# Layer 2's delta rule: products with beta made ahead of the chunk loop

## The chip, the cores and the metric

The kernel runs on one core of a Trainium2 chip. The metric is the time of one execution on the device in microseconds (us); the time of the kernel before is the median of three runs. One more execution was recorded by the hardware profiler, and all rows and durations below come from that one. The core's engines are called as the profile calls them: PE (TensorE, matmuls; PEld are its weight loads), DVE (VectorE), ACT (ScalarE), POOL (GpSimd), and SP, which issues DMAs.

## The reference, cut to what matters

The model has four layers of attention and feed-forward, for 8 sequences of 256 tokens with 128 features. The change touches the attention of layer 2 alone, a gated delta rule over chunks of 32 tokens, for 4 heads of width 32:

```python
q, k = _l2norm(q), _l2norm(k)
v, k_beta = v * beta[..., None], k * beta[..., None]
A = where(strict_lower, k_beta @ k.T, 0)            # per chunk
attn_inv = inverse of (eye + A)                     # lower triangular, 32 x 32
u = attn_inv @ v
w = attn_inv @ k_beta
def step(S, inp):                                   # over the 8 chunks of a sequence
    q_i, k_i, u_i, w_i = inp
    attn_local = where(incl_lower, q_i @ k_i.T, 0)
    u_t = u_i - w_i @ S
    o_i = q_i @ S + attn_local @ u_t
    return S + k_i.T @ u_t, o_i
S0 = zeros
```

Its output (delta) is mixed with two causal filters of v (a short one of 5 taps, a long one of 64) and with v itself, by gates that a small network computes from x and from statistics of the four paths. The result is normalised, multiplied by a matrix and added to the residual.

## The kernel before, in words

After the first layer the batch is split into two halves, a and b, of four sequences (1024 tokens) each. `run` emits the stages of the halves in a written order; stage 7 is layer 2's attention (`l2_attn`, L1219 to L1476), once for a and once for b. Beside a's stage 7 the program puts the layer 1 experts of half b (L1027 to L1048), beside b's stage 7 the layer 3 experts of half a (L1598 to L1616). The framework's scheduler merges what is emitted: each engine has one queue in order, and the scheduler fixes that order when the program is built, what was emitted first having precedence. `keep_pace` ties the experts to the stage beside them: `step` collects matmuls of the stage as marks, 16 of them in `l2_attn` (8 of the Gram products, L1294, and 8 of the chunk loop, L1367), and the first matmuls of expert unit i of 16 stand on PE behind mark int(0.8 i).

Within `l2_attn` the data of a half are held as [128, 1024] tiles. In the "H" layout (vH, kH, dH) a partition is head and token within the chunk, the columns are sequence, chunk and feature; in the "T" layout (vT, kT, kq) a partition is head and feature. A transpose of 32 x 32 blocks on DVE leads from one to the other. `heads` (L1242) makes a product for each of the four heads, 32 x 32, on four parts of PE's array. An f32 product stands in the profile as two PE records with two weight loads; 4 sequences x 4 heads are then 32 records of each.

The steps, in order:

- Front (L1249 to L1282): normalisation of tokens, projections, causal convolutions, l2 norms, beta = sigmoid.
- Gram products (L1284 to L1302): nb is the mask "below" times beta on DVE (L1286), then times -1 on POOL (L1287). For each of 8 chunks PE makes k k^T and k q^T into one of four PSUM buffers; DVE writes nm = product x nb (L1295) and loc = product x "upto" (L1298).
- FIR (L1310 to L1322): the long filter, 768 records of small matmuls.
- Inverse (L1326 to L1339): 31 rows of forward substitution on DVE, two operations each (L1334, L1335), while PE runs experts. Then an ACT copy (L1336), a DVE transpose (L1338) and an ACT copy with a strided read into inv (L1339), which holds the transposed inverse X.
- Chunk loop (L1356 to L1385): a state of [128, 4 x 32], cleared by a memset. Per chunk: PE ks = k S; DVE r = v - ks (L1369) and r = r x beta (L1370); PE us = X r; DVE copies u (L1375); PE os = q S + loc u, which ACT copies to dH (L1380); PE ss = k^T u; DVE adds it to the state (L1385). The last chunk makes no ss.
- Gates (L1387 to L1476): statistics of the four paths on ACT and DVE, of which those of the filters and v run beside the chunk loop; then the gate network on PE, softmax, mixing, norm, output product, and the addition to x (L1476).

Of the kernel before, what the change touches and what calls it, by code (L numbers as in the profile page):

```python
# [8 lines left out]
F32 = mybir.dt.float32  # L9
# [3 lines left out]
ALU = mybir.AluOpType  # L13
# [3 lines left out]
P = 128  # L17
B, S, D = 8, 256, 128
# [858 lines left out]
class Half(Chip):  # L877
# [341 lines left out]
    def l2_attn(self):  # L1219
# [3 lines left out]
        nc, tc, B, T, NT = self.nc, self.tc, self.B, self.T, self.NT  # L1223
        NC, NB = S // 32, T // 32
        wide = lambda r: r.unsqueeze(2).to_broadcast([P, NB, 32])
        blk = lambda z: z.rearrange("p (j d) -> p j d", d=32)
        by_bn = lambda z: z.rearrange("p (b n d) -> p b n d", n=NC, d=32)
        by_b = lambda z: z.rearrange("p (b s) -> p b s", s=S)
        with ExitStack() as ctx:
# [4 lines left out]
            vH, fsH, flH, dH = big("vH"), big("fsH"), big("flH"), big("dH")  # L1234
            beta = one.tile([P, NB], F32, name="beta", tag="beta")

            with ExitStack() as cm:
                mid = cm.enter_context(self.sb("l2m"))
                vT, kH, loc, inv = big("vT", mid), big("kH", mid), big("loc", mid), big("inv", mid)
                kq = mid.tile([P, 2, T], F32, name="kq", tag="kq")  # L1240

                def heads(out, weights, moving, start=True, stop=True):  # L1242

                    for h in range(4):
                        r = slice(32 * h, 32 * h + 32)
                        mm = nc.tensor.matmul(out[r], weights[r], moving[r], start=start, stop=stop)
                    return mm

                with ExitStack() as c2:  # L1249
                    tmp = c2.enter_context(self.sb("l2t"))  # L1250
                    psum = c2.enter_context(self.ps("l2aps", 4))
                    xn = tmp.tile([P, NT, D], F32, name="xn", tag="xn")
# [4 lines left out]
                    for j, dst in enumerate((vT, kT, qT, bT)):  # L1257
                        for g in range(T // 512):
                            c = slice(512 * g, 512 * g + 512)
                            ps = psum.tile([P, 512], F32, name="proj", tag="m")  # L1260
# [22 lines left out]

                    below, upto = self.const("below", tmp), self.const("upto", tmp)  # L1284
                    nb = big("bT", tmp)
                    nc.vector.tensor_tensor(blk(nb), below.unsqueeze(1).to_broadcast([P, NB, 32]), wide(beta), ALU.mult)  # L1286
                    nc.gpsimd.tensor_scalar(nb, nb, -1.0, None, ALU.mult)  # L1287
                    nm = tmp.tile([P, 32, B, NC], F32, name="nm", tag="xn")
                    for n in range(NC):
                        ps = psum.tile([P, B, 2, 32], F32, name="gram", tag="m")  # L1290
# [13 lines left out]
                with ExitStack() as c2:  # L1304
# [31 lines left out]
                    nc.scalar.copy(nm, xt.rearrange("p s c -> p c s"))  # L1336
                    xc = tmp.tile([P, 32, NB], F32, name="xc", tag="xmat")
                    nc.vector.transpose(xc.rearrange("p c j -> p (c j)"), nm.rearrange("p c s -> p (c s)"))  # L1338
                    nc.scalar.copy(blk(inv), xc.rearrange("p c j -> p j c"))  # L1339

                    fT = big("fT", tmp)
                    short = w["taps"][:, 12:17]
# [10 lines left out]
                wk = cm.enter_context(self.sb("l2gw"))  # L1353


                with ExitStack() as c2:  # L1356
                    tmp = c2.enter_context(self.sb("l2r", 2))
                    psum = c2.enter_context(self.ps("l2rps", 1))
                    st = mid.tile([P, B, 32], F32, name="state", tag="state")
                    nc.vector.memset(st, 0.0)  # L1360
                    for n in range(NC):
                        kn, xn, qn, ln, hn = (by_bn(z)[:, :, n, :] for z in (kq[:, 0, :], inv, kq[:, 1, :], loc, kH))
                        bn = beta.rearrange("p (b n) -> p b n", n=NC)[:, :, n].unsqueeze(2).to_broadcast([P, B, 32])
                        ps = psum.tile([P, B, 32], F32, name="ks", tag="ks")
                        for b in range(B):
                            mm = heads(ps[:, b], kn[:, b], st[:, b])
                        self.step(mm)  # L1367
                        r = tmp.tile([P, B, 32], F32, name="r", tag="r")
                        nc.vector.tensor_tensor(r, by_bn(vH)[:, :, n, :], ps, ALU.subtract)  # L1369
                        nc.vector.tensor_tensor(r, r, bn, ALU.mult)  # L1370
                        ps = psum.tile([P, B, 32], F32, name="us", tag="us")
                        for b in range(B):
                            heads(ps[:, b], xn[:, b], r[:, b])
                        u = tmp.tile([P, B, 32], F32, name="u", tag="u")
                        nc.vector.tensor_copy(u, ps)  # L1375
                        ps = psum.tile([P, B, 32], F32, name="os", tag="os")
                        for b in range(B):
                            heads(ps[:, b], qn[:, b], st[:, b], stop=False)
                            heads(ps[:, b], ln[:, b], u[:, b], start=False)
                        nc.scalar.copy(by_bn(dH)[:, :, n, :], ps)  # L1380
                        if n < NC - 1:
                            ps = psum.tile([P, B, 32], F32, name="ss", tag="ss")
                            for b in range(B):
                                heads(ps[:, b], hn[:, b], u[:, b])
                            nc.vector.tensor_tensor(st, st, ps, ALU.add)  # L1385

                paths = (fsH, flH, dH, vH)  # L1387
                sH = gates.tile([P, NB, 32], F32, name="sH", tag="sH")
# [515 lines left out]
```

## Time and profile before

| | |
|---|---|
| median of three runs (their range) | 2854.66 us (2846.88 to 2856.15) |
| the profiled execution's own time | 2850.54 us |
| its span, first to last instruction | 2848.7 us |
| PE busy, matmul instructions | 2347.8 us, 17346 |
| DVE busy, instructions | 1602.1 us, 3704 |
| ACT busy, instructions | 1022.8 us, 1750 |
| POOL busy, instructions | 318.9 us, 441 |
| mean granted PE clock | 0.883 |

The two executions of layer 2's attention, in us from the span's start:

| | half a | half b |
|---|---|---|
| first Gram product | 1231.8 | 1534.6 |
| row of X copied into inv by ACT begins | 1310.2 | 1601.3 |
| first us of the chunk loop | 1312.2 | 1603.3 |
| end of the last os | 1359.4 | 1646.7 |
| last addition to x (L1476) begins | 1427.3 (the first at 1424.8) | 1709.3 |

How to read it: the 2.0 us between the time of the profiled execution and its span lie outside the instructions. A row of a timeline gives start, duration, engine, line, operation, tiles, count, and in brackets how long the engine was idle before it and what ended that. "issue" stands for idle time in which the engine waited for nothing that the profile shows. A row of waits says who waited for whom, the sum in us, how often, and the longest. A row of busy time by stretch gives the stretch, its length, busy time (and count of instructions) of PE, PEld, DVE, ACT and POOL, the granted PE clock, the DMA engines' busy share and GB/s. A busy PE is not a PE at its peak, since matmuls overlap; starts of successive matmuls say more than durations.

### The profile page before, as it was taken

How to read it: one execution, taken by the hardware profiler on the slowest of the kernel's cores; microseconds unless marked ns; L12 is line 12 of the kernel's file. 1: busy time of each engine (PE TensorE's matmuls, PEld its weight loads, DVE VectorE, ACT ScalarE, POOL GpSimd, SP SyncE). 2: the span in 40 equal slices, each digit the busy share in tenths (PEclk: the TensorE clock that was granted, in tenths of full speed). 3: DMA queues.
4: the chain of work that ended last, by engine and by line, in shares of the span. 5: the costliest groups of instructions: out<-in, count | busy, mean ns of one | idle time of the engine just before them, and what ended most of it. 6: DMA issues, size and time to landing. Idle time of an engine off the chain costs nothing. (4 is left out here: it accounts for less than half of the span.)

```text
span 2848.7 us, 42771 instructions
## 1 busy us (share of the span) xinstructions
PE 2347.8 (82%) x17346; PEld 1553.0 (55%) x17346; DVE 1602.1 (56%) x3704; ACT 1022.8 (36%) x1750; POOL 318.9 (11%) x441
## 2 busy tenths in 40 slices
PE   5784788578789879858895898999698798779999
PEld 3672455367455445445463656666465565545666
DVE  6536443653558988777558754544553644463432
ACT  1021333211349578335542335222234421224322
POOL 0372110047000000000000000000201000210000
PEclk8695799679799989968996899999899899879999
DMA  7133331513200000100010001000221000030100
GB/s 256 22 45 103 103 90 44 194 25 41 79 15 24 9 29 17 31 27 22 12 40 24 17 23 50 1 16 16 59 55 37 27 8 16 26 91 4 43 23 23
DMA packets 103027, 127.27 MB, mean 45 GB/s; under 512 B 15161, under 2 KB 84094, under 8 KB 97726
## 3 DMA queue, kind: packets, MB, share of 16 engines
q1 hardware_dynamic: 61706, 71.56, 8.4%
q10 hardware_dynamic: 28836, 43.28, 4.5%
q0 software_dynamic: 12288, 9.71, 2.5%
q8 instruction: 136, 2.23, 0.3%
q14 instruction: 61, 0.50, 0.1%
HBM read 96.84 MB, written 27.53 MB: 44 GB/s over the span
## 5 line engine op out<-in xcount | busy, mean ns | idle before, releaser
L1610 PEld LDWEIGHTS po<-w_e,hT 128*128 128x128 f32 x2048 | 265.4, 198 | 71.5 <-issue 48.5
L1610 PE MATMUL po<-w_e,hT 128*128 128x128 f32 x2048 | 288.2, 286 | 11.1 <-DVE hT L1604 7.6
L1598 PE MATMUL ph<-x2T,w_e 128*128 128x512 f32 x512 | 264.0, 620 | 5.8 <-ACT hT L1606 4.9
L1606 ACT ACTIVATE hT<-ph,w_l_cols 128x512 f32<-128x512 f32 x192 | 131.3, 686 | 323.1 <-PE ph L1598 319.0
L621 DVE TENSOR_REDUCE nm<-sc 128x3 f32<-128x384 f32 (+1 forms) x192 | 130.4, 689 | 126.4 <-PE sc L619 125.3
L1040 PEld LDWEIGHTS po<-w_e,hT 128*128 128x128 f32 x1024 | 135.3, 197 | 75.9 <-DVE hT L1033 29.4
L658 ACT ACTIVATE pr_e<-scT 128x384 f32<-128x384 f32 (+1 forms) x192 | 111.3, 597 | 171.1 <-PE scT L655 164.2
L1040 PE MATMUL po<-w_e,hT 128*128 128x128 f32 x1024 | 144.8, 286 | 14.3 <-DVE hT L1033 8.6
L1030 PE MATMUL pu<-xnT,w_e 128*128 128x512 f32 x256 | 139.2, 626 | 9.3 <-ACT gs L1032 9.3
L1027 PE MATMUL pg<-xnT,w_e 128*128 128x512 f32 x256 | 138.6, 624 | 0.8 <-ACT prT L223 0.7
L1616 DVE SCALAR_TENSOR_TENSOR x_res<-po,gt,x_res 128x128 f32<-128x128 f32 x256 | 79.4, 358 | 100.8 <-PE po L1610 100.3
L231 PE MATMUL tp<-c_ident,xn 128*128 128x128 f32 x208 | 53.3, 380 | 93.3 <-DVE xn L251 85.6
L500 ACT ACTIVATE gs<-pg 128x512 f32<-128x512 f32 x64 | 38.2, 597 | 249.6 <-PE pg L495 249.6
L1033 DVE SCALAR_TENSOR_TENSOR hT<-pu,w_l_bias,gs 128x512 f32<-128x512 f32 x128 | 95.0, 745 | 57.7 <-PE pu L1030 54.8
L1598 PEld LDWEIGHTS ph<-x2T,w_e 128*128 128x128 f32 x512 | 84.6, 195 | 68.9 <-ACT hT L1606 33.2
L1032 ACT ACTIVATE gs<-pg,w_l_bias 128x512 f32<-128x512 f32 x128 | 87.2, 689 | 96.4 <-PE pg L1027 86.4
L668 PE MATMUL ctx<-pr_e,vz 128*32 128x256 f32 x512 | 106.6, 395 | 2.8 <-ACT pr_e L658 2.8
L1756 DVE TENSOR_TENSOR gw<-sc,dec 128x768 f32<-128x768 f32 x64 | 61.2, 957 | 84.3 <-PE sc L1750 83.9
L513 POOL DMA_INDIRECT l_acc<-eo,idx x64 | 101.9, 1592 | 34.9 <-DVE eo L512 16.9
L617 PE MATMUL sc<-ks,qs 72*128 72x256 bf16 x256 | 75.8, 296 | 28.7 <-DMA ks<-l_parts 17.4
L1046 ACT ACTIVATE ys<-po,pr 128x128 f32<-128x128 f32 x256 | 73.3, 368 | 65.3 <-PE po L1040 64.5
L231 PEld LDWEIGHTS tp<-c_ident,xn 128*128 128x128 f32 x208 | 33.9, 170 | 112.4 <-DVE xn L251 85.5
(604 smaller groups left out, 4998.5 us busy)
## 6 DMA issues: line engine op xcount, KB each, us to landing
l_parts<-sT SPq DMA_DIRECT2D x48, 192.0 KB, 5.0
qs<-l_parts SPq DMA_DIRECT2D x16, 576.0 KB
w_l_wu<-in_l_wu ACTq DMA_DIRECT2D x8, 1024.0 KB
w_e<-in_l_e SPq DMA_DIRECT2D x16, 512.0 KB, 3.4
w_e<-in_l_e ACTq DMA_DIRECT2D x16, 512.0 KB, 4.0
w_e<-in_l_e SPq DMA_DIRECT2D x16, 384.0 KB, 3.2
w_e<-in_l_e ACTq DMA_DIRECT2D x16, 384.0 KB, 3.1
l_parts<-sT ACTq DMA_DIRECT2D x24, 192.0 KB, 4.0
```

The source lines that it names most:

```text
L513: nc.gpsimd.indirect_dma_start(out=accs[h][:, :], out_offset=bass.IndirectOffsetOnAxis(ap=idx[:, j : j + 1], axis=0), in_=eo[:, h, :], in_ ...
L621: nc.vector.tensor_reduce(blocks[:, hp * pr : hp * pr + hp, :], sc[:, :, 0:384].rearrange("p h (k t) -> p h k t", t=P), AX.X, ALU.max, neg ...
L658: nc.scalar.activation(pe, sc[:, :, 0:384], AF.Exp, scale=float(1.0 / np.sqrt(np.float32(8.0))))
L668: nc.tensor.matmul(o, z, pe[:, 0:S], start=(j == 0), stop=False)
L1027: mm = nc.tensor.matmul(pg, wg[:, c], xnT[:, cols], start=True, stop=True)
L1030: self.keep_pace(nc.tensor.matmul(pu, wu[:, c], xnT[:, cols], start=True, stop=True), part)
L1032: nc.scalar.activation(gs, pg, AF.Silu, bias=w["l1_bias"][:, 0, e, k : k + 1])
L1033: nc.vector.scalar_tensor_tensor(hT[:, k, :], pu, w["l1_bias"][:, 1, e, k : k + 1], gs, ALU.add, ALU.mult)
L1040: nc.tensor.matmul(po[:, i, :], hT[:, k, i * P : (i + 1) * P], wd[:, k * P : (k + 1) * P], start=(k == 0), stop=(k == 1),)
L1598: mm = nc.tensor.matmul(ps, we[:, k * P : (k + 1) * P], xnew[:, 512 * g : 512 * g + 512], start=True, stop=True)
L1606: nc.scalar.activation(hT[:, k, :], ps, AF.Relu, bias=bias)
L1610: nc.tensor.matmul(po[:, i, :], hT[:, k, i * P : (i + 1) * P], we[:, (4 + k) * P : (5 + k) * P], start=(k == 0), stop=(k == 3),)
```

## The change

The equations are turned. With X the inverse, u_t = X (beta v) - X (beta k) S. The factor beta goes into X's columns once, as X is stored (on DVE, in place of ACT's copy). From this X beta, the loop makes z (X beta k, transposed, as weights for the product with S) and y = X beta v for two chunks at a time in one PSUM buffer "zy", ahead of the first chunk of each pair; DVE copies z over the place of k in kq, ACT copies y over vT, which are no longer needed by then. None of these depends on the state. What then remains of a chunk is us = z S, u = y - us on DVE, ss = k^T u (now emitted ahead of os), os and the addition to the state. The first chunk takes u = y, and has no products with the empty state, so that no memset is needed; the state after it is a copy of ss. The mark of the first chunk becomes the last product of the first zy, that of the others the last us. The sign of the Gram mask is put on beta (32 columns, DVE) in place of the whole mask (1024 columns, POOL).

```diff
                     nb = big("bT", tmp)
-                    nc.vector.tensor_tensor(blk(nb), below.unsqueeze(1).to_broadcast([P, NB, 32]), wide(beta), ALU.mult)
-                    nc.gpsimd.tensor_scalar(nb, nb, -1.0, None, ALU.mult)
+                    less = tmp.tile([P, NB], F32, name="less", tag="less")
+                    nc.vector.tensor_scalar(less, beta, -1.0, None, ALU.mult)
+                    nc.vector.tensor_tensor(blk(nb), below.unsqueeze(1).to_broadcast([P, NB, 32]), wide(less), ALU.mult)
...
-                    nc.scalar.copy(blk(inv), xc.rearrange("p c j -> p j c"))
+                    nc.vector.tensor_tensor(blk(inv), xc.rearrange("p c j -> p j c"), wide(beta), ALU.mult)
...
+                zT, y = kq[:, 0, :], vT
...
-                    nc.vector.memset(st, 0.0)
                     for n in range(NC):
-                        kn, xn, qn, ln, hn = (by_bn(z)[:, :, n, :] for z in (kq[:, 0, :], inv, kq[:, 1, :], loc, kH))
-                        bn = beta.rearrange("p (b n) -> p b n", n=NC)[:, :, n].unsqueeze(2).to_broadcast([P, B, 32])
-                        ps = psum.tile([P, B, 32], F32, name="ks", tag="ks")
-                        for b in range(B):
-                            mm = heads(ps[:, b], kn[:, b], st[:, b])
+                        if n % 2 == 0:
+                            ps = psum.tile([P, B, 2, 2, 32], F32, name="zy", tag="zy")
+                            for b in range(B):
+                                for j in range(2):
+                                    xn = by_bn(inv)[:, b, n + j, :]
+                                    heads(ps[:, b, j, 0], by_bn(kH)[:, b, n + j, :], xn)
+                                    mm = heads(ps[:, b, j, 1], xn, by_bn(vH)[:, b, n + j, :])
+                            nc.vector.tensor_copy(by_bn(zT)[:, :, n : n + 2, :], ps[:, :, :, 0, :])
+                            nc.scalar.copy(by_bn(y)[:, :, n : n + 2, :], ps[:, :, :, 1, :])
+                        zn, yn, qn, ln, hn = (by_bn(z)[:, :, n, :] for z in (zT, y, kq[:, 1, :], loc, kH))
+                        u = yn
+                        if n:
+                            ps = psum.tile([P, B, 32], F32, name="us", tag="us")
+                            for b in range(B):
+                                mm = heads(ps[:, b], zn[:, b], st[:, b])
+                            u = tmp.tile([P, B, 32], F32, name="u", tag="u")
+                            nc.vector.tensor_tensor(u, yn, ps, ALU.subtract)
                         self.step(mm)
-                        r = tmp.tile([P, B, 32], F32, name="r", tag="r")
-                        nc.vector.tensor_tensor(r, by_bn(vH)[:, :, n, :], ps, ALU.subtract)
-                        nc.vector.tensor_tensor(r, r, bn, ALU.mult)
-                        ps = psum.tile([P, B, 32], F32, name="us", tag="us")
-                        for b in range(B):
-                            heads(ps[:, b], xn[:, b], r[:, b])
-                        u = tmp.tile([P, B, 32], F32, name="u", tag="u")
-                        nc.vector.tensor_copy(u, ps)
+                        if n < NC - 1:
+                            ss = psum.tile([P, B, 32], F32, name="ss", tag="ss")
+                            for b in range(B):
+                                heads(ss[:, b], hn[:, b], u[:, b])
                         ps = psum.tile([P, B, 32], F32, name="os", tag="os")
                         for b in range(B):
-                            heads(ps[:, b], qn[:, b], st[:, b], stop=False)
-                            heads(ps[:, b], ln[:, b], u[:, b], start=False)
+                            if n:
+                                heads(ps[:, b], qn[:, b], st[:, b], stop=False)
+                            heads(ps[:, b], ln[:, b], u[:, b], start=n == 0)
                         nc.scalar.copy(by_bn(dH)[:, :, n, :], ps)
-                        if n < NC - 1:
-                            ps = psum.tile([P, B, 32], F32, name="ss", tag="ss")
-                            for b in range(B):
-                                heads(ps[:, b], hn[:, b], u[:, b])
-                            nc.vector.tensor_tensor(st, st, ps, ALU.add)
+                        if n == 0:
+                            nc.vector.tensor_copy(st, ss)
+                        elif n < NC - 1:
+                            nc.vector.tensor_tensor(st, st, ss, ALU.add)
```

## The prediction

> **What bounds the kernel now.** I read the page for the span, then the busy time by stretch around the two executions of layer 2's attention (one for each half of the batch, a and b), then the timelines of TensorE (PE) and VectorE (DVE) there, the waits, and the instruction queue among the DMAs. The chain of waits reaches back only to about 2000 us, so it says nothing of this stage; the stretches have to.
>
> ```profile
> span 2848.7 us, 42771 instructions
> ...
> q8 instruction: 136, 2.23, 0.3%
> ```
> ```profile
> 1246.60:1269.60 23.00, 14.94 (x780) 13.27 (x778) 12.53 (x38) 3.19 (x6) 0.00 (x0) 0.62 0.15 39
> 1312.10:1359.40 47.30, 38.91 (x1275) 26.51 (x1275) 30.25 (x68) 25.10 (x48) 0.00 (x0) 0.71 0.04 12
> 1359.40:1425.00 65.60, 57.01 (x200) 29.59 (x201) 37.83 (x54) 36.00 (x64) 1.97 (x1) 0.97 0.05 13
> ...
> 1603.30:1646.80 43.50, 33.92 (x1289) 25.68 (x1290) 28.77 (x71) 16.32 (x28) 0.00 (x0) 0.84 0.05 16
> 1646.80:1710.00 63.20, 59.39 (x235) 34.75 (x236) 35.01 (x63) 25.13 (x34) 1.97 (x1) 0.95 0.05 17
> 1710.00:1743.00 33.00, 33.00 (x189) 23.32 (x188) 12.51 (x44) 9.14 (x14) 0.00 (x0) 1.00 0.00 0
> ```
>
> The columns are stretch, length, busy PE, weight loads, DVE, ACT, POOL, granted clock, DMA. Rows 2 and 4 are the chunk loop of a and b (47.3 and 43.5 us for 8 chunks), rows 3 and 5 the gates and output after it. Half a's layer ends at 1425 us, at the same time as the last experts that run beside it, and PE has some 8.6 us of room in row 3. Half b's layer ends at 1710 us, but PE goes on with the other half's experts, 33.00 of 33.00 us busy in row 6, and the next stage of b follows only after them. So time saved in a counts when the chain or PE is shorter; in b only less idle PE counts.
>
> ```profile
> 1345.79 0.29 DVE L1369 TENSOR_TENSOR r<-vH,ks 128x128 f32<-128x128 f32 x1 [0.86 <-PE ks L1246]
> 1346.11 0.29 DVE L1370 TENSOR_TENSOR r<-r,beta 128x128 f32<-128x128 f32 x1
> 1347.14 0.29 DVE L1375 COPY u<-us 128x128 f32<-128x128 f32 x1 [0.73 <-PE us L1246]
> ...
> 1349.53 0.28 DVE L1385 TENSOR_TENSOR state<-state,ss 128x128 f32<-128x128 f32 x1
> ```
>
> One chunk: three trips between PE and DVE, four DVE operations, about 5 us. What PE does in the waits is expert work, queued there by the order of the program.
>
> ```profile
> 1249.02 1.81 PE L1246 MATMUL fl<-vH,fw 32*32 32x32 f32 x127 [0.83 <-issue]
> 1252.34 1.91 PE L1246 MATMUL fl<-vH,fw 32*32 32x28 f32 x128 [1.52 <-issue]
> 1256.07 0.62 PE L1246 MATMUL fl<-vH,fw 32*32 32x24 f32 x29 [1.81 <-issue]
> ```
>
> This row decides most. In the FIR products, independent small matmuls like those of the chunk loop, PE runs about 128 of them and then stands up to 1.8 us with nothing to wait for. With their weight loads that is 256 instructions. The page's instruction queue fits: 2.23 MB in 136 packets is 16.4 KB each, and PE's 2 x 17346 instructions over 136 packets are 255 each. The packet starts in the trace lie 3.3 to 3.9 us apart in this stretch, and nowhere in the run closer than 3.3. A stream of small matmuls is therefore bound at 3.3 to 3.9 us per 128 records, not by the 14 ns each that PE takes (32 records of "us" in 0.45 us).
>
> **The change part by part.** Each f32 product is two records, so 4 sequences x 4 heads are 32 records a chunk, and each step below is per half.
>
> *Sign on beta.* The front of the stage stands on DVE:
>
> ```profile
> DVE nm L1295 <- POOL bT L1287: 3.0, 1, 3.0
> DVE nm L1295 <- PE gram L1246: 2.0, 1, 2.0
> ```
>
> (half a; b has the first line alike without the second.) The 2.77 us POOL operation goes; a DVE one on 32 columns comes (0.14 us, as beta + 1 in L1280). That frees 2.8 us, but the Gram products are late next: four buffers hold 128 records, and the rest needs the next block of instructions. In a, the last Gram product already made DVE wait 2.0 us; starting the second batch earlier by 2.8 us cannot bring a block closer than 3.3 us after the last. I take 1.5 us (ends 0.5 and 2.8). PE has almost nothing to do then, so this counts in both halves: 3 us.
>
> *Beta into the inverse.* L1339 was an ACT copy with a strided read:
>
> ```profile
> L1339 ACT COPY inv<-xc x2: 1968/1976/1983, 1310.2 to 1601.3; 128x1024 f32<-128x1024 f32 x2
> ```
>
> DVE does it with beta. A product of this size with a broadcast is 1.22 us (L1403); a strided side cost L1295 0.37 against 0.27 for L1298, so 1.2 to 1.7. I take 1.4, a gain of 0.6 us; the ends are a gain of 0.8 and, with one 1.2 us statistic queued ahead on DVE, a loss of 0.9. It also waits no longer for a busy ACT.
>
> *The loop's operations.* Gone: ks (8 x 32 records), us in its old form (256), 32 of os for the first state, and on DVE 8 x 0.29 for r, 8 x 0.29 for r x beta, 8 x 0.29 for the copy of u, one of seven adds turned into a copy, and the memset of 0.17. New: z 256 and y 256 records, 7 x 32 for us, 7 subtractions of 0.29 on DVE; four zT evictions of 256 columns on DVE (0.29 for 128, 0.67 for 512 columns in L221: 0.42 each) and four of y on ACT, about 0.4 each, between the 0.27 us of L1380 for 128 and the 0.59 of L223 for 512 columns. DVE, with the inverse: 7.1 us before; 2.0 + 1.7 + 1.4 = 5.1 after. PE: 256+256+512+224 = 1248 records before, 256+256+224+480+224 = 1440 after, so +192, or +2.7 us at 14 ns.
>
> *The chain per chunk.* Three trips become two (us to u, ss to state), and ss goes ahead of os, whose 64 records fill a wait. From the timeline: 0.45 us, 0.3, 0.29, 0.3, then 0.45, 0.3, 0.29, 0.2: some 2.6 us bare. With the experts' pieces between, 3.2; eight chunks and 2.5 us for the first z and y give 28 us by chain alone.
>
> *What is late next.* Here the Trainium skill speaks: its page "Runtime: NRT & Kernel Launch", section on instruction fetch mechanics, says that PE's instructions come in blocks of 256 while the current block executes, and that crossing a block is mostly hidden. By that the 192 extra records cost 2.7 us and the loops could come near 28 us: 19 + 15 us off the two. The rows above say otherwise for small matmuls: up to 1.8 us of open stall per block. I go by the row. 1440 records are 2880 instructions, 11.25 blocks, 37 to 42 us at 3.3 to 3.75 us, before any expert work lies between. Before, the loop of a held 1275 records, 10.0 blocks, 33 to 37 us: b's 43.5 us were already near that, and one wait of 1.2 us in it has "issue" as its cause. A rule of "TensorE: Matmul & The Clock Gate" (section "Wait — 56ns, not 53.3ns?") speaks against the change too: a small matmul's start costs 25 ns at least, 4.8 us for the 192; the 14 ns of this trace hold instead, with products on different parts of the array.
>
> With 50 expert records left between, 11.6 blocks at 3.6 us: I take 42 us for each loop (ends 37 and 46). Before, each loop held about 13.5 us of experts (in a 48 of 0.11 and 19 of 0.43, start to start at full clock); with one wait fewer per chunk and z and y in the others I expect 8, so 5.5 us of experts move behind the loop.
>
> *Sum, by what PE does.* Loop of a before: 1208 x 0.014 + 13.5 = 30.4 us of work, so 16.9 of 47.3 us were idle or at half clock; b: 30.5, so 13.0. After, at 42 us: 20.2 + 8, so 13.8 lost. Half a: 16.9 - 13.8 = 3.1 less loss, - 2.7 for the new records, + 2.1 for the front and the inverse; of the 8.6 us of room in row 3, 0 to 3.6 can be used, since the tail now starts 7.4 us earlier (5.3 + 2.1) and its end isn't the limit. I take 1.8: 4.3 us gained. Half b: 13.0 - 13.8 - 2.7 + 2.1 = -1.4, and 0 to 3 of the 3.8 us left in row 5: +0.1 at the middle. Together 4.4 us: span 2844, profiled time 2846 where it had 2850.54. Against the median of 2854.66 that is 2850. What comes later keeps its work; the program's scheduling lays its order out anew, which no row prices: 4 us either way, as far as the two executions' equal loops differ (47.3 and 43.5). The marks that pace the experts don't bind: when a's inverse was done, 8 of the 16 units beside it had begun, and the first mark that moves is unit 10's.
>
> **The rivals.**
> *The chain is all.* Fetching hides as the page says; loops of 32 us lose 4 each. Then a gains 16.9 - 4 - 2.7 + 2.1 + 3.6 = 15.9, b 13.0 - 4 - 2.7 + 2.1 = 8.4: 2830. For it: clocks of 0.71 and 0.84 in the loops, PE waits for DVE of 5.6 and 7.3 us in them. Against: the FIR rows. Chance 0.13.
> *Fetch at its quickest.* Blocks 3.3 us apart, loops of 37.5 us, lost 9.3: a 16.9 - 9.3 - 2.7 + 2.1 + 1.8 = 8.8, b 13.0 - 9.3 - 2.7 + 2.1 = 3.1: 2843. For: five of six blocks in the second FIR stretch came at 3.3 to 3.8. Against: in the two loops only one block of some twenty came within 3.4 us of the last. Chance 0.21.
> *Fetch takes more than it gives (slower).* Its place is the loop of b and the stretch to 1743. If the scheduling puts few experts between, PE stands in the stalls: loop 46 us with 4 of experts, 21.8 lost. Then b is 13.0 - 21.8 - 2.7 + 2.1 + 3 = 6.4 later, a 16.9 - 21.8 - 2.7 + 2.1 + 3.6 = 1.9: 2863. It decides from about 44 us with under 6 us of experts between, where the sum passes zero. For: the stall already in b's loop; z and y come in bursts of 128, one block each. Against: list order still fills PE's waits. Chance 0.26.
> *The change doesn't reach the end*, as in the sum: main case, chance 0.40.
>
> **How the numbers follow.** About 0.3% (8.6 us) is what a measurement of this kernel can tell from no change. The main case gives 2850, with its own range 2846 to 2858. The first two rivals are the faster chance, 0.34 (the part of the second within 0.3% and the main case's part beyond it cancel); same 0.40; slower 0.26, with the new order of later layers in it. 2836 to 2864 leaves out most of the first rival and the far end of the third, about 2 in 10.
>
> **What would show it.** DVE's wait for POOL at L1295 is gone, a wait of about 1 to 2 us for Gram stays. The loop from first zy to last os takes 39 to 46 us per half; PE waits with cause "issue" in it, up to 1.8 us each, and instruction packets 3.3 to 3.9 us apart. Fewer expert records lie in it than 1275 - 1208 = 67 in a. Half a's output at about 1420, the end of the experts beside b, with all shifts, 3 to 7 us before 1743. Wrong if loops fall under 37 us, if no "issue" waits appear, or if the end of the experts beside b moves by more than 10 us.

## The result and the profile after

The change made the kernel slightly slower: 2859.26 us at the median of 20 runs (2852.46 to 2866.32), against 2854.70 us for 20 runs of the kernel before (2843.84 to 2859.60). The ratio is 1.0026 with a 95% interval of 1.0015 to 1.0036. The medians differ by 4.6 us; the ratio, which is taken over all the runs, stands for 7.4 us. The forecast was 4.4 us faster. The profiled execution took 2860.8 us.

The page of the changed kernel, first line and instruction queue:

```profile
span 2858.4 us, 43539 instructions
...
q8 instruction: 139, 2.28, 0.3%
```

768 instructions and 3 packets more: 384 matmul records (17730 where there were 17346), 192 per half as counted, with as many weight loads. Busy time by stretch of the changed kernel (same columns as before), rows 1 and 3 the chunk loops of a and b, rows 2 and 4 what follows each:

```profile
1310.20:1356.80 46.60, 31.57 (x1469) 24.02 (x1469) 27.00 (x54) 21.51 (x37) 0.00 (x0) 0.71 0.04 13
1356.80:1425.00 68.20, 59.02 (x203) 31.07 (x204) 39.07 (x64) 36.80 (x63) 1.97 (x1) 0.92 0.04 12
1608.60:1651.10 42.50, 26.59 (x1468) 22.29 (x1467) 25.12 (x52) 15.08 (x26) 0.00 (x0) 0.72 0.02 5
1651.10:1714.00 62.90, 59.67 (x256) 34.80 (x250) 36.01 (x69) 25.41 (x34) 1.97 (x1) 0.97 0.05 17
```

The loops take 46.5 and 42.6 us where they took 47.2 and 43.4: one round trip between PE and DVE less per chunk has bought 0.7 and 0.8 us. Of the 1469 and 1468 records, 1440 are the layer's own, so 29 and 27 are experts, where there were 67 and 81. PE is busy for 7.3 us less in each loop, and in b the granted clock has fallen from 0.84 to 0.72.

What PE waited for in the changed kernel, first half a's loop, then half b's (from some 5 us ahead of each loop on; of the 2.5 us for hT, 0.9 lie ahead of b's):

```profile
PE zy L1246 <- issue: 7.3, 4, 2.7
PE os L1246 <- issue: 3.4, 2, 1.8
PE pu L1030 <- ACT gs L1032: 2.8, 1, 2.8
PE us L1246 <- issue: 1.3, 1, 1.3
```
```profile
PE zy L1246 <- issue: 9.0, 5, 2.4
PE os L1246 <- issue: 3.6, 4, 1.3
PE ph L1609 <- ACT hT L1617: 2.5, 2, 1.6
PE ss L1246 <- issue: 0.8, 1, 0.8
```

Before, PE waited there for DVE, 5.6 us in a; these two rows of a's waits are the larger part of it.

```profile
PE us L1246 <- DVE r L1370: 2.3, 2, 1.6
...
PE os L1246 <- DVE u L1375: 1.8, 3, 0.7
```

The waits for DVE are down to fractions of a us, and 12.0 and 13.4 us of "issue" stand in their place. The packets of the instruction queue start at 1311.4, 1318.5, 1322.6, 1326.4, 1329.7, 1333.2, 1336.8, 1340.6, 1344.1, 1348.6 and 1352.8 in a's loop. The first step, 7.1 us, holds the 2.8 us wait for ACT; the others are 3.3 to 4.5 us. The stalls keep the same step: they end at 1332.07, 1335.81, 1339.54, 1343.00 and 1346.73, and between each of these times and the next PE's records in the trace, matmuls and weight loads together, number exactly 256. PE's timeline shows one such place:

```profile
1333.06 0.65 PE L1246 MATMUL ss<-u,kH 32*32 32x32 f32 x32
1333.51 0.31 PE L1246 MATMUL os<-u,loc 32*32 32x32 f32 x8
1333.62 0.31 PE L1246 MATMUL os<-state,kq 32*32 32x32 f32 x8
...
1335.81 0.27 PE L1246 MATMUL os<-u,loc 32*32 32x32 f32 x4 [1.85 <-issue]
...
1336.85 0.65 PE L1246 MATMUL us<-state,kq 32*32 32x32 f32 x32 [0.18 <-DVE state L1396]
```

The profile shows no wait for a result in the 1.85 us.

At the front, DVE's wait for POOL (3.0 us in each half) is gone; in a the only wait of that kind left is this row, where the Gram products were 2.0 us late before.

```profile
DVE nm L1296 <- PE gram L1246: 1.0, 1, 1.0
```

Then where is the loss? In the experts that run beside a. One line's instructions on PE, their output products from 1300 us to 1445 us (the two times are the first and last start), before and after:

```profile
L1040 PE MATMUL po<-w_e,hT x192: 272/275/582, 1300.1 to 1422.5; 128*128 128x128 f32 x192
```
```profile
L1040 PE MATMUL po<-w_e,hT x168: 272/275/582, 1299.7 to 1437.3; 128*128 128x128 f32 x168
```

They end 15 us later, although a's own layer ends 3 us earlier (its last output product starts at 1423.8, not 1426.8). Half b's next layers need the results of these experts. The first Gram product of half b comes at 1540.8 where it came at 1534.6. Counted from the first projection of a's layer, which starts at a slightly different time in every execution, that is 342.4 us where it was 335.1: 7.3 us late. From there to the end of the experts beside b it is 217.0 us where it was 212.1, another 4.9 us. Then comes the feed-forward of half b's layer 2 (last product in L1213): from its end to the end of the span it is 1074 us where it was 1077. So the loss lies between a's layer and that point, and nothing is lost behind it.

### The profile page after: what moved, and what is told of

Its sections match the earlier page's. It is cut to its first block, busy times and chain, and to the rows that moved or that the text cites. A ratio compares the mean times of both kernels' runs of the same rounds, so it can differ in the third digit from the quotient of the medians.

```text
span 2858.4 us, 43539 instructions
## 1 busy us (share of the span) xinstructions
PE 2345.0 (82%) x17730; PEld 1554.5 (54%) x17730; DVE 1601.6 (56%) x3680; ACT 1029.7 (36%) x1762; POOL 313.1 (11%) x439
## 5 line engine op out<-in xcount | busy, mean ns | idle before, releaser
L1040 PEld LDWEIGHTS po<-w_e,hT 128*128 128x128 f32 x1024 | 136.4, 199 | 77.1 <-DVE hT L1033 33.4
L1040 PE MATMUL po<-w_e,hT 128*128 128x128 f32 x1024 | 145.8, 287 | 13.7 <-DVE hT L1033 11.5
L1030 PE MATMUL pu<-xnT,w_e 128*128 128x512 f32 x256 | 138.4, 623 | 12.9 <-ACT gs L1032 12.9
L1027 PE MATMUL pg<-xnT,w_e 128*128 128x512 f32 x256 | 137.2, 619 | 0.0
L1046 ACT ACTIVATE ys<-po,pr 128x128 f32<-128x128 f32 x256 | 72.9, 367 | 55.2 <-PE po L1040 54.2
```

Source lines behind the costliest of these rows:

```text
L1027: mm = nc.tensor.matmul(pg, wg[:, c], xnT[:, cols], start=True, stop=True)
L1030: self.keep_pace(nc.tensor.matmul(pu, wu[:, c], xnT[:, cols], start=True, stop=True), part)
L1040: nc.tensor.matmul(po[:, i, :], hT[:, k, i * P : (i + 1) * P], wd[:, k * P : (k + 1) * P], start=(k == 0), stop=(k == 1),)
```

## The experiments

Theory A: the small products are bound by their instruction blocks, so the shorter chain cannot shorten the loop, and the experts that stood in the old loop's waits are pushed behind it, where they end late. Theory B: the loss comes from the added instructions wherever the experts stand. Theory C: it comes from something beside the loop (the front, a new order of instructions in the layers behind it). A loop is counted from the first us (in the changed loops zy) to the end of the last os. "Experts' end", "a's end" and "b's Gram" in the table are starts of the last expert product, a's last output product and b's first Gram product, from the first projection of a's layer, in one execution of each kernel.

| kernel | ratio, 95% interval | loops a, b (us) | blocks in the built loops | expert products in the built loops | experts' end | a's end | b's Gram |
|---|---|---|---|---|---|---|---|
| before | 1 | 47.2, 43.4 | 10.0, 10.1 | 33, 40 | 223.0 | 227.3 | 335.1 |
| the change | 1.0026, 1.0015 to 1.0036 | 46.5, 42.6 | 11.5, 11.5 | 14, 13 | 238.9 | 225.4 | 342.4 |
| sign alone | 0.9979, 0.9964 to 0.9995 | 44.7, 42.9 | 10.0, 10.1 | 33, 40 | 219.7 | 224.0 | 331.9 |
| change without sign | 1.0027, 1.0014 to 1.0041 | 47.6, 42.6 | 11.5, 11.5 | 14, 13 | 238.5 | 225.0 | 342.0 |
| three trips, shortened | 0.9979, 0.9965 to 0.9993 | 39.7, 39.5 | 9.6, 9.8 | 23, 32 | 217.4 | 215.8 | 333.3 |
| more products | 1.0020, 1.0001 to 1.0039 | 49.1, 48.3 | 11.5, 11.7 | 34, 49 | 225.2 | 229.1 | 335.4 |
| z and y joined | 0.9944, 0.9920 to 0.9967 | 33.4, 35.7 | 9.4, 9.5 | 12, 14 | 220.9 | 207.4 | 324.4 |
| change, seven ties | 1.0016, 0.9998 to 1.0033 | 56.2, 56.7 | 12.0, 12.2 | 45, 58 | 224.4 | 232.5 | 338.3 |
| joined, seven ties | 1.0004, 0.9988 to 1.0020 | 57.2, 55.2 | 10.0, 10.2 | 46, 58 | 223.8 | 231.9 | 335.1 |
| sign alone, seven ties | 0.9985, 0.9973 to 0.9998 | 59.9, 59.5 | 10.4, 10.6 | 59, 75 | 213.7 | 235.2 | 334.3 |
| change in a alone | 1.0011, 0.9997 to 1.0025 | 46.7, 42.4 | 11.5, 10.1 | 14, 40 | 238.3 | 224.8 | 341.8 |
| change in b alone | 0.9979, 0.9967 to 0.9991 | 45.2, 39.9 | 10.0, 11.5 | 33, 13 | 221.0 | 224.9 | 328.2 |
| change, one tie | 1.0073, 1.0046 to 1.0099 | 52.3, 55.3 | 11.8, 12.1 | 36, 53 | 230.6 | 229.9 | 345.4 |

Blocks are products x 2 records x 2 instructions / 256; an expert product is two records too.

**The sign alone.** The kernel before with only this:

```diff
-                    nc.vector.tensor_tensor(blk(nb), ..., wide(beta), ALU.mult)
-                    nc.gpsimd.tensor_scalar(nb, nb, -1.0, None, ALU.mult)
+                    nc.vector.tensor_scalar(less, beta, -1.0, None, ALU.mult)
+                    nc.vector.tensor_tensor(blk(nb), ..., wide(less), ALU.mult)
```

> The kernel before with the sign on beta alone. PE's queue stands in the same order as before in the Gram products, the FIR and both chunk loops. My theory (the slowdown comes from the chunk loop, which holds more blocks of PE instructions and fewer experts): the front of the stage is 2 to 4 us shorter in each half and both loops stay at 47 and 43 us, so 4 to 6 us faster than before, about 2849. Rival (something in the front, or the mere new order of later layers, made the change slow): no gain, or 3 us and more slower.

2844.48 us against 2849.62: 5 to 6 us faster, as expected. From first Gram product to first FIR product it takes 12.6 and 11.5 us where it took 14.9 and 13.9.

**The change without the sign.** The change with those lines undone:

```diff
-                    nc.vector.tensor_tensor(blk(nb), ..., wide(less), ALU.mult)
+                    nc.vector.tensor_tensor(blk(nb), ..., wide(beta), ALU.mult)
+                    nc.gpsimd.tensor_scalar(nb, nb, -1.0, None, ALU.mult)
```

> The change with the sign put back on POOL as before, so the loop's edits (z and y, two trips, no empty state, beta in the inverse) alone. PE's queue has the change's order. If the two parts add up: the sign alone gave 0.21%, the whole change costs 0.26%, so this one is 8 to 14 us slower than before (0.3 to 0.5%). If the front's gain is lost in the changed kernel because something else comes late there: as slow as the change, 4 to 5 us over before.

2859.62 us against 2852.99, ratio 1.0027, the same as the whole change: the second of the two cases, and the parts don't add up. The front does take 12.9 and 14.0 us again, some 2 us more than in the change (10.9 and 11.8), but the experts' end stays at 238.5. So within the change the sign is worth nothing that can be measured, though alone it is worth 5 us. That half b then waits for the experts, which a shorter front doesn't move, fits this, but is not shown by itself.

**Three trips, shortened.** The sign, beta in the inverse, ss ahead of os and no products with the empty state, but ks, us and ss as before, without z and y. Against the loop of before:

```diff
-                        nc.vector.tensor_tensor(r, r, bn, ALU.mult)
...
+                        r = by_bn(vH)[:, :, n, :]
+                        if n:
+                            ps = psum.tile([P, B, 32], F32, name="ks", tag="ks")
...
```

> The sign, beta in the stored inverse, no products with the empty state and ss ahead of os, but no z and y: r = v - k S, u = X beta r, three trips a chunk as before. By the built order each loop then holds 592 small products (before 604, the change 720), 9.6 and 9.8 blocks of 256 PE instructions, and 23 and 32 expert products, 9.5 and 9.0 us of work (before 33 and 40, 13 us; the change 14 and 13, 6.3 and 4.1 us). My theory: loops of about 40 us, PE time lost in them about 14 us each against 16.9 and 13.0 before; with the front's 5 us some 6 to 9 us faster than before, 2846 to 2849. Rival (the shorter chain is what counts): no faster than the kernel with the sign alone.

2843.65 us against 2849.62, at the near end of what was expected and no better than the sign alone, as the rival had it. The loops are 39.7 and 39.5 us with three trips per chunk, 7 and 3 us shorter than the change's with two, and have 0.4 and 1.6 us of "issue". So three trips at 9.6 blocks are shorter than two trips at 11.5. b's Gram, though, came no earlier than with the sign alone, so the shorter loop in a did not show in the time; why, stays open.

**More products.** The kernel before with each us product of six chunks made twice (the first result is overwritten by the same value), so that the loop has 700 small products, near the change's 720.

```diff
-                            heads(ps[:, b], xn[:, b], r[:, b])
+                            for _ in range(2 if n < 6 else 1):
+                                heads(ps[:, b], xn[:, b], r[:, b])
```

> The kernel before with us made twice in six of eight chunks (the second time over the first, same values): 96 products more a loop, 700 in place of 604, 11.5 and 11.7 blocks as in the change, but with 34 and 49 expert products (13.9 and 15.3 us) still in the loops and POOL's sign as before. If the count of small products alone makes the change slow: 8 to 11 us slower than before (1.5 blocks of 3.6 us in each half), 2863 to 2866. If it is the experts that the change drives out of the loops: only the 1.3 us of PE work a half and some stall, 2 to 6 us slower, 2857 to 2861.

2859.16 us against 2849.62, 9.5 us by the medians and 5.7 by the ratio of 1.0020, whose interval of 0.3 to 11 us covers both forecasts. The trace says more. The loops grew by 2 and 5 us, the experts stayed in them (34 and 49), the experts' end is 2.2 us later and b's Gram within 0.3 us of before. 9 us were lost only later, in the feed-forward of half b's layer 2: 34.3 us from the end of the experts beside b to its last product, where it was 25.6. PE's products stand there, and up to the end of the program, in the same order as before. What differs is the granted clock (the first row is the kernel before, the second this one, the third the change in half a alone, below):

```profile
1746.40:1772.00 25.60, 20.84 (x111) 14.22 (x110) 13.58 (x41) 21.62 (x28) 5.10 (x5) 1.00 0.20 70
1747.00:1781.30 34.30, 29.53 (x111) 20.40 (x110) 14.13 (x41) 23.91 (x33) 5.13 (x5) 0.73 0.16 53
1745.50:1779.10 33.60, 29.11 (x112) 20.22 (x111) 13.59 (x41) 23.53 (x32) 5.13 (x5) 0.74 0.17 54
```

So added instructions alone do not move the experts, which speaks against B for half a. What this execution lost, it lost to the clock in a later layer; why the clock was low there, and whether the other executions lost time in the same place, is not known.

**z and y joined.** The change, with k and v of a chunk side by side, so that one product with 64 columns makes both; z is then transposed on DVE. 592 small products in place of 720.

```diff
+                    kv = mid.tile([P, 2, B, NC, 32], F32, name="kv", tag="kv")
+                    for j, z in enumerate((kH, vH)):
+                        nc.scalar.copy(kv[:, j].rearrange("p b n d -> p (b n d)"), z)
...
-                                    xn = by_bn(inv)[:, b, n + j, :]
-                                    heads(ps[:, b, j, 0], by_bn(kH)[:, b, n + j, :], xn)
-                                    mm = heads(ps[:, b, j, 1], xn, by_bn(vH)[:, b, n + j, :])
-                            nc.vector.tensor_copy(by_bn(zT)[:, :, n : n + 2, :], ps[:, :, :, 0, :])
+                                    mm = heads(ps[:, :, b, j, :], by_bn(inv)[:, b, n + j, :], kv[:, :, b, n + j, :])
+                            nc.vector.tensor_copy(zH, ps[:, 0].rearrange("p b j d -> p (b j d)"))
+                            nc.vector.transpose(zT[:, n * B * 32 : (n + 2) * B * 32], zH)
```

> The change, but z and y come from one product of 64 columns (X beta as weights, k and v side by side, copied there by ACT during the inverse), and DVE transposes z: 592 small products a loop in place of 720, 9.4 blocks in place of 11.5. Expert products in the loops stay few (12 and 14, 5.2 and 4.4 us). If blocks of instructions set the loop's length: loops of 34 to 37 us where the change has 46 and 42, and 8 to 12 us faster than the change, 2847 to 2851. If displaced experts are all that costs and the blocks don't matter: as slow as the change, 2857 to 2860.

2834.41 us against 2849.62, ratio 0.9944: faster than both kernels, and the fastest of all. By the ratios it is 23 us faster than the change, where 8 to 12 were expected. Its loops and what follows a's:

```profile
1304.10:1337.60 33.50, 25.54 (x1209) 20.08 (x1210) 27.80 (x58) 20.32 (x36) 0.00 (x0) 0.80 0.05 16
1337.60:1404.00 66.40, 57.45 (x203) 30.68 (x204) 38.42 (x62) 37.62 (x61) 1.97 (x1) 0.95 0.04 13
1587.00:1622.70 35.70, 25.97 (x1214) 20.91 (x1213) 26.34 (x56) 14.96 (x26) 0.00 (x0) 0.76 0.02 4
```

It has as few experts in its loops as the change, and the same two trips. On PE only the number of products, and with it of blocks, is smaller: 9.4 blocks instead of 11.5, and the loops are 13 and 7 us shorter, although DVE has the transposes on top. 9.4 blocks in 33.4 us are 3.55 us each, the spacing of the packets. The waits of PE in a's loop are mostly for data again, "issue" is down to 1.7 us:

```profile
PE ss L1246 <- DVE u L1385: 2.2, 3, 1.2
PE us L1246 <- DVE state L1400: 1.7, 2, 1.4
PE os L1246 <- issue: 1.3, 1, 1.3
```

The experts take as long behind the loop as in the change (80.0 us, 1337.6 to 1417.6), but the loop ends that much earlier: their last product is at 220.9, near the 223.0 of before, and a's layer ends 20 us earlier.

**Ties.** Three kernels in which seven expert products per half are tied in the built order behind one chunk each, so that the experts stand between the chunks again. The ties add no waits; they only fix the order on PE.

```diff
+    def pin(self, inst, unit, place):
+        m = self.pins.get((unit, place)) if self.pinned else None
+        if m is not None:
+            dep = mybir.DependencyInfo(mybir.DependencyClass.NoSync, mybir.DependencyReason.DATA)
+            self.tc.add_manual_dep(self.pace[m], inst.ins.name, dep, reason="experts between the chunks")
...
+                        self.pin(mu, G * e + g, f"k{k}")
...
+                    self.pin(mo, G * e + g, "po")
```

The marks are numbers 9 to 15, one per chunk after the first.

> The change, but the program ties expert products of the other half between the chunks: marks 9 to 15 of the loop stand on PE behind products of expert units 8 to 10 (half a) or 5 to 7 (half b). By the built order the loops hold 45 and 58 expert products, 18.2 and 19.2 us of work, where the change has 14 and 13 (6.3 and 4.1 us); small products stay 720, blocks go from 11.5 to 12.0 and 12.2. My theory (the experts that the loop no longer takes are what makes the change slow, and they fit into the stalls between blocks): loops 43 to 48 us, the last experts beside a end near 1425 instead of 1437.6, 8 to 14 us faster than the change, so 3 to 9 us faster than before. Rival (blocks alone): 1 to 4 us slower than the change.

The change with seven ties: 2859.35 us against 2852.99, ratio 1.0016, where 8 to 14 us less than the change was expected. By the ratios it is 3 us faster than the change, so both forecasts missed. The experts did come back to 224.4, but the loops grew:

```profile
1303.00:1359.20 56.20, 45.08 (x1531) 31.11 (x1531) 31.92 (x61) 28.63 (x54) 0.00 (x0) 0.82 0.06 18
1598.10:1654.80 56.70, 45.40 (x1558) 34.54 (x1557) 30.30 (x67) 19.11 (x32) 0.00 (x0) 0.82 0.04 13
```

with these waits as the longest in a's loop (the line numbers of this kernel are higher; L1048 is L1030 of the change):

```profile
PE pu L1048 <- ACT gs L1052: 2.8, 1, 2.8
PE po L1060 <- DVE hT L1053: 2.0, 1, 2.0
PE us L1267 <- issue: 1.9, 2, 1.2
```

Now the chain stands behind the experts, with the experts' own waits for ACT and DVE in it.

> Joint z and y product (592 small products a loop) together with the same ties: 46 and 58 expert products in the loops (19 us each), 10.0 and 10.2 blocks. My theory: loops of 38 to 42 us, PE almost without stall in them, 2 to 6 us faster than the joint product alone, so 17 to 22 us under before. If the joint loop's room is used up already or the ties delay its chain: no faster than the joint product alone, or up to 5 us slower than it.

The joined kernel with the ties: 2854.34 us, some 17 us slower by the ratios (1.0004 and 0.9944) than without, outside both forecasts, for the same reason: 57.2 and 55.2 us of loop.

> Control: the kernel before with the sign on beta and the same ties. Its loop took 13 us of experts by itself; with the ties 25 us, in 10.4 and 10.6 blocks. If ties help only where the loop had lost its experts: within 3 us of the kernel with the sign alone, or slower, as the chain of three trips now waits for experts. If ties help any kernel: 5 us and more faster than the sign alone.

The control, the sign alone with the ties: 2847.50 us, ratio 0.9985, near the sign alone. Its loops are 15 and 17 us longer than the sign alone's, with 59 and 75 expert products in them, and most of what is lost there comes back behind: the experts end 6 us earlier, and b's Gram is 2.4 us later.

**Half by half.** The whole change in one half's layer, the other half's layer as before.

```diff
+                if self.tag == "a":
                     with ExitStack() as c2:
...
+                else:
+                    with ExitStack() as c2:
...
```

The first branch is the loop of the change, the second that of before; the sign and the store of X are switched in the same way, and "b" takes the place of "a" in the second kernel.

> The whole change in half a's layer alone; half b's layer is that of the kernel before. If the loss is made in half a (five to seven us by which the change's trace shows half b's Gram products late, because the experts beside a end 15 us later), this kernel is 5 to 8 us slower than the kernel before (ratio 1.0018 to 1.0028) and its trace has half b's first Gram product 5 to 9 us later than before, counted from the start of half a's layer; half b's loop stays at about 43 us. If half a is neutral and all comes from half b, it is within 2 us of before.

2855.87 us against 2851.44: 1.0011, less than expected at the middle, with the lower end of the forecast inside its interval. The trace has what was expected: b's Gram at 341.8, 6.7 us late, and b's loop at 42.4 us. It also has 8 us at the low clock in half b's feed-forward (the third row under "More products"), with the products in the order of before; that part of its loss is not the late experts'.

> The whole change in half b's layer alone; half a's layer is that of the kernel before. If each half carries its own loss, the trace has half b's first Gram product where it was before and the end of the experts beside b 4 to 6 us later, and the time is 3 to 5 us above before (ratio 1.0010 to 1.0018). If the loss is all made in half a, it is within 2 us of before. A sum of the two halves' changes far from the whole change's 7 us would say that the newly laid order of later layers has a hand in it.

2845.58 us against 2851.44: 0.9979, 6 us faster than before and outside both cases. From b's Gram to the experts' end it is 212.7 us, within 0.6 us of before; b's loop takes 39.9 us with 9.8 us of "issue", in the whole change 42.6 with 13.4, in the same form. What it gained lies ahead of b's layer (b's Gram at 328.2), where the code is that of before but PE's order is not quite (328 of the 380 records from a's end to b's Gram match), and where the granted clock was 0.92 and 1.00 (1426 to 1470 and 1470 to 1500 us) against 0.88 and 0.94. So the 4.9 us that half b lost in the trace of the whole change are not a fixed price of it.

**One tie.** The change with one tied expert product per half, which leaves 36 and 53 expert products in the loops. In the table of ties:

```diff
-    5: {(8, "po"): 9, (9, "k0"): 10, (9, "k1"): 11, (9, "po"): 12, (10, "k0"): 13, (10, "k1"): 14, (10, "po"): 15},
...
+PINS = {5: {(9, "k0"): 9}, 9: {(5, "o3"): 9}}
```

> The change with one expert product per half tied behind the loop's first chunk, so that the built order has 36 and 53 expert products in the two loops, near the 33 and 40 of the kernel before, where the change has 14 and 13. If the displaced experts alone make the loss and the seven ties of the earlier kernel were only too many, it is 3 to 8 us faster than the change, at or a little below the kernel before, with loops of 48 to 52 us. If the added instructions make the loss wherever the experts stand, the loops grow by as much as the experts take (50 to 56 us) and the time stays within 2 us of the change (ratio 1.0015 to 1.003).

2871.76 us against 2851.44 (six runs): 1.0073, the slowest, and a miss of both theories' times. The loops are 52.3 and 55.3 us, as the second expected; the experts end 8 us earlier than in the change, but a's end is 4.5 us later, and b's Gram comes at 345.4, 3 us later than in the change. So here experts that end earlier did not bring b's Gram forward. What makes this kernel the slowest stays open.

## Why the prediction was wrong, step by step

- *Blocks bind the small products.* Right. "Issue" stalls of up to 2.7 us, packets 3.3 to 4.5 us apart, exactly 256 instructions from stall to stall, and the loop follows the number of blocks once the chain is shorter: the joined kernel with 9.4 blocks shows it. That the fetch is mostly hidden, as the Trainium skill's page "Runtime: NRT & Kernel Launch" has it in its section on instruction fetch mechanics, would have given loops near 28 to 32 us; measured were 46.5 and 42.6. For this stream the row was the better guide.
- *Loop of 42 us.* b's was 42.6, a's 46.5. In a, 11.5 blocks took 4.0 us each; without the 2.8 us for which one expert product inside waited for ACT, with the chain behind it, 3.8, near b's 3.7. That b's loop came so close is in part luck: the same loop took 39.9 us in the kernel with the change in b alone.
- *Front, 1.5 us a half.* Too small: 4.0 and 2.1 us in the change. The Gram products hardly became late: DVE waits 1.0 us for them in a, where it had waited 2.0. It did not count in the end, as the kernel without the sign shows.
- *14 ns a record.* Too much at the full clock. The 0.45 us for 32 records of us take in the last record's own 0.19; their starts are 8 ns apart where the granted clock was 1.0, and 14 where it was 0.5. At the full clock the 192 new records are 1.6 us and not 2.7, too little to turn the sum.
- *8 us of experts left in each loop, 5.5 us pushed out.* 14 and 13 expert products were left, 6.3 and 4.1 us by the same durations (0.22 us for a po product, 0.86 for a wide one), so 7 and 9 us were pushed out. The trace has z and y products among the chunk's own instead (those that start at 1347.08, for one).
- *"Of the 8.6 us of room in row 3, 0 to 3.6 can be used".* This step failed, and with it the sign of the forecast. The sum took PE's idle time behind a's loop for room that the pushed-out experts could fill, and half a's own layer for the thing to be shortened. But that idle time was the experts' own: of the 8.6 us, 7.7 were waits of expert products for DVE and ACT; ahead of the longest, DVE was at the mixing of the gates (L1459, L1461). These are PE's longest waits behind a's loop (to 1425 us), before and after:

```profile
PE po L1040 <- DVE hT L1033: 3.7, 1, 3.7
PE pu L1030 <- ACT gs L1032: 2.1, 2, 1.4
PE po L1040 <- ACT ys L1046: 1.9, 1, 1.9
```
```profile
PE po L1040 <- DVE hT L1033: 5.2, 2, 4.9
PE pu L1030 <- ACT gs L1032: 3.5, 3, 1.5
PE po L1040 <- ACT ys L1046: 0.6, 2, 0.4
```

More experts in that stretch brought more such waits, 9.3 us. The gate network also has precedence on PE: for 17 us on end all its products are the gates' (L1433 to L1437, in the changed kernel L1444 to L1448). Each pair of rows holds the last expert product of L1027 ahead of the gates and the first behind them, before and after:

```profile
1370.86 1.02 PE L1027 MATMUL pg<-xnT,w_e 128*128 128x512 f32 x2
1396.25 1.02 PE L1027 MATMUL pg<-xnT,w_e 128*128 128x512 f32 x2
```
```profile
1362.67 1.12 PE L1027 MATMUL pg<-xnT,w_e 128*128 128x512 f32 x2
1389.66 1.02 PE L1027 MATMUL pg<-xnT,w_e 128*128 128x512 f32 x2
```

In the changed kernel the last seven units beside a start at 1355.1, 1362.7, then 1392.5, 1398.4, 1411.3, 1416.6 and 1426.1; before, of the last six, three started ahead of the gates (1357.6, 1363.9, 1368.9) and three after them (1396.3, 1400.8, 1407.9). From the loop's end to the experts' end it takes 80.8 us (1356.8 to 1437.6) where it took 63.4 (1359.4 to 1422.8). Of these 17 us, 9 are the experts themselves (179 records on PE where there were 141; the 7 us above hold at the full clock, and part of them ran at half of it, 1404.2 to 1411.0), 6 are a's output products and the first of its feed-forward, which now come ahead of the last experts, and the rest is mostly idle time. The loop ended only 2.6 us earlier, so nothing made up for it.
- *Half b, +0.1 us.* 4.9 us were lost in the trace of the whole change and 0.6 in the kernel with half b alone. By the prediction's own sum, 42.6 us of loop less 20.2 and 4.1 of work is 18.3 lost, not 13.8; and with 39.9 us, 15.6.
- *The rival "fetch takes more than it gives"* came nearest: it had loops of 46 us with 4 us of experts in them, and 2863 us; measured were 46.5 us with 6.3 in a, 42.6 with 4.1 in b, and 2859. Its place was wrong: it put most of the loss in b, and b alone lost nothing. It also granted a 3.6 us of the same room.

Two things are shown. Fewer products pay, by the joined kernel. And the change makes the experts beside a end late: in the three traces with its loop in a (the change, the change without sign, the change in a alone) they end at 238.3 to 238.9 and b's Gram comes at 341.8 to 342.4; in the three with the old loop in a (before, the sign alone, the change in b alone) the experts end at 219.7 to 223.0 and b's Gram comes at 328.2 to 335.1. The latter differ among themselves by as much as before and the change do.

That the late experts are the whole cause is not shown. Bringing them back by ties lengthened the loop and gained at most a part, and with one tie b's Gram was later still. The halves don't add up either: 1.0011 and 0.9979 make 0.9990, against 1.0026 for the whole. The difference of 0.36% is uncertain by about 0.2% from the three intervals, so it may be part noise. The order of the layers behind half b's is not behind it: from the end of the experts beside b, PE's products come in the order of before in every kernel, but for a few at the start, and from the end of half b's feed-forward to the end of the program it is 1073 to 1082 us in all 13 traces. What is left are the order between a's end and b's Gram, where blocks begin, and the granted clock, which alone made 8 to 9 us in two of the traces; which of these it is stays open.

## What to carry to other kernels

Before splitting small matmuls to shorten a chain, count the stage's PE instructions (products x records x 2) and divide by 256: where the profile shows "issue" stalls in a stream of small products, expect the stage to last at least that many blocks at the spacing of the instruction packets (here no two packets of PE's queue were less than 3.2 us apart in any of the 13 traces), however short the chain is. A chain's waits may be holding other work; a faster chain, or more products to fill it, evicts that work, so look for where it goes and who waits for its end. Idle time of PE is room for that work only if the work itself is not what PE is waiting for. If the same result can be had with fewer, wider products, take that first: here it turned 0.26% of loss into 0.56% of gain.

## What the runs showed of the hardware

The stalls at block ends were known from the FIR products, which are independent; that they appear alike in a loop of dependent chunks with experts between, and cost more in it (up to 2.7 us, against 1.8), was not expected.

The granted clock was low in these loops: 0.71 and 0.72 in the change, 0.80 and 0.76 in the joined kernel, 0.82 with the ties. That the stalls lower it is not shown: before, a's loop had 0.71 too, with no "issue" among its waits.

Records of 32 x 32 products on different parts of the array started 14 ns apart where the granted clock was 0.5 (32 records of us within 0.42 us from 1336.85), and 8 ns apart where it was 1.0 (within 0.26 us from 1354.33). Even at 14 ns the loop's 1440 records come to 20.2 us of the 46.5 and 42.6, so PE's own pace was not what set its length.
